# A two-layer graph-attention kernel: the aggregation of five heads as one-pass products of split factors, with the order of work dealt anew

## The chip, the core and the metric

The kernel runs on one core of a Trainium2 chip. The metric is the time of one execution on the device, in microseconds; lower is better. The engines that matter are TensorE (matrix products, with a separate instruction that loads the stationary operand), VectorE, ScalarE, GpSimd, and the DMA queues, of which SP's and GpSimd's are used here.

## The reference

Two layers of graph attention, a residual and a layer norm, over 512 nodes with 768 features. The first layer has eight heads, the second has one.

```python
def gat_layer(x, W, a_s, a_d, b, edge_index, concat):
    n = x.shape[0]
    H, C = a_s.shape
    h = (x @ W).reshape(n, H, C)
    src, dst = (edge_index[0], edge_index[1])
    alpha_s = jnp.einsum('nhc,hc->nh', h, a_s)
    alpha_d = jnp.einsum('nhc,hc->nh', h, a_d)
    e = jax.nn.leaky_relu(alpha_s[src] + alpha_d[dst], NEG_SLOPE)
    m = jax.ops.segment_max(e, dst, num_segments=n)
    e = jnp.exp(e - m[dst])
    denom = jax.ops.segment_sum(e, dst, num_segments=n)
    alpha = e / (denom[dst] + EPS)
    msg = h[src] * alpha[:, :, None]
    out = jax.ops.segment_sum(msg, dst, num_segments=n)
    ...
```

After layer 1 (768 to 8 x 768) comes an ELU, then layer 2 (6144 to 768), then the input is added and every row normalised. The kernel makes a dense 512 x 512 attention matrix out of the edges, so that the sum over messages becomes a matrix product.

## The kernel before

All matrices are 32-bit floats. For each head h there are three families of products on TensorE:

- the projection `M.P*` of the head after the next one (x times that head's part of W1): 15 products instead of 18, by sums and differences of blocks in thirds (`by_thirds`, line 472), four matmuls of 128x128 by 256 columns each;
- the aggregation (`mixed`, line 986): the features `HS[h]` (512 nodes x 768) times the attention matrix, held turned in `PT` (512 x 512). Seven half-size products P1 to P7 are made instead of eight, for three column blocks c, two matmuls each: tokens such as `P50` (product P5, block 0). They need sums of blocks of both factors, made by VectorE: `l0` to `l3` (`left_sums`, into `gS`) and `r0` to `r3` (`right_sums`, into `pS`). The result passes through an ELU into `gT` by ScalarE and VectorE (`fork`, `u`, `w`, `x`, `y`, `n`, `nn`, `N`, `b`, `B`, `f`, `F`);
- the second layer's product `m.P*` (`gT` times that head's part of W2), again 15 products (`second_thirds`, line 552); VectorE adds each to `h2` by `e.P*` (line 560). The sums of `gT` are `g.P*` (`g_thirds`, line 586), some in the spare room of `gS`.

Beside them run, for each next head: logits (`src`, `dst`, VectorE line 422), softmax (`row`, `lift`, `leak`, `rank`, `att`), turning the attention matrix by DMA (`out0` to `out3` are `turn_out`, `in0` to `in3` are `turn_in`), the loads of weights (`d.*` for W1 of the head after next, `t.*` for W2 of the next), the sums of weight blocks (`T.*`, `w.*`, line 200, and additions by GpSimd's DMA queue, line 187), and `back`, which loads sums of x from DRAM into `gT`, since room in the on-chip memory is short.

The order of work is written out by hand. A script is a string of tokens; each token issues its instructions on their engines in the script's order, and each engine works through its own queue in that order. `HEAD[...]` + `SECOND[...]` + `NEXT[...]` make one head; heads 1 to 5 share a script. Buffers come from pools: a tile that is allocated again waits until the last reader of the tile before it in that slot has ended. Products accumulate in PSUM banks that are handed out from a list (`mm`).

The lines of the aggregation's products and of the projection's eviction, which the profile names:

```python
nc.tensor.matmul(st[bank][:, :HN], A_[p][:, k, c * P:(c + 1) * P], B_[p][:, k, :],
                 start=start and k == 0, stop=k == 1, skip_group_check=True)
...
nc.scalar.activation(out(o), ps, AF.Copy, scale=how)
```

Of the kernel before, what the change touches and what calls it, by code (L numbers as in the profile page):

```python
# [8 lines left out]
F32 = mybir.dt.float32  # L9
# [28 lines left out]
def gat_pass(  # L38
# [349 lines left out]
    def left(aT, s):  # L388
# [360 lines left out]
    XA, xsums = left(xT, xS)  # L749
# [161 lines left out]
    parted = {}  # L911

    def turn_out(q, t, rden=None):
        if rden is not None:
            nc.scalar.activation(q, q, AF.Copy, scale=rden)  # L915
        apart = pS[:, t].rearrange("p k n -> p (k n)") if t < 3 else work.tile([P, N], F32, name="nr")
        apart = apart.bitcast(U16)
# [4 lines left out]
    def turn_in(t, copy=nc.scalar.copy):  # L922
        copy(PT.rearrange("p s n -> p (s n)").bitcast(U16).rearrange("p (s n h) -> p s n h", s=NT, h=2)[  # L923
# [25 lines left out]
    def left_sums(h):  # L949
        hs = HS[h]  # L950
        a11, a12, a21, a22 = hs[:, :2, L], hs[:, 2:, L], hs[:, :2, R], hs[:, 2:, R]
        room = xS if h + 1 == H else gS
        s1, s2, s4 = (room.rearrange("p a k n -> p a (k n)")[:, j, :].rearrange("p (k n) -> p k n", k=2)
                      for j in range(3))
# [8 lines left out]
    def right_sums():  # L963
        b11, b12, b21, b22 = PT[:, :2, near], PT[:, :2, far_], PT[:, 2:, near], PT[:, 2:, far_]
        t1, t2, t4 = pS[:, 0], pS[:, 1], pS[:, 2]
# [6 lines left out]
        ]  # L972

    def mixed(h, A_, B_):

        ops = {}
        for c in range(HK):
# [16 lines left out]
            def keep_copy(name, st=st):  # L994
                def f():
                    st[name] = work.tile([P, HN], F32, name=name)
                    nc.scalar.copy(st[name], st["B"][:, :HN])  # L997
                return f
# [11 lines left out]
            def corner(st=st, j=near_j, c=c):  # L1010
                st["nl"] = work.tile([P, HN], F32, name="nl")
                st["zl"] = work.tile([P, HN], F32, name="zl")
# [69 lines left out]

    AA, lsums = left_sums(0)
# [55 lines left out]
    def hold():  # L1139
        forks.extend(mm.tiles.pop() for _ in range(2))  # L1140

    HEAD = ["""d.p12 hold banks P10 fork0 P50 P60 u0 src2 P20 n0 src3 P70 w0 row d.r2 d.r3 d.r1 d.r4 d.r0 d.r5 d.P14 d.p13 d.P13
        d.P12 nn0 d.P1 x0 P11 fork1 P40 b0 P30 y0 f0 P51 dst3 N0 P61 u1 P21 n1 P71 B0 w1 dst2 x1 nn1 N1 P12 fork2 P41 P22 b1
        P31 B1 y1 n2 nn2 P62 F0 u2 N2 w.0 P52 f1 P72 F1 w2 x2 m.P1.0 w.1 P42 lift2 lift0 b2 P32 leak0 m.k0 lift1 m.P1.1 B2 y2
        f2 zero rank0""",
        """P10 P50 w.P10 fork0 src0 P60 u0 P20 src1 n0 row w.P2 P70 w0 x0 nn0 N0 P11 w.P0 fork1 P40 b0 d.r0 d.r1 d.r2 d.r3 d.P1
        d.r4 d.r5 w.P6 d.P14 d.p13 d.P13 d.p12 P30 d.P12 y0 f0 dst0 B0 P51 P61 u1 F0 P21 n1 P71 w1 x1 nn1 dst1 N1 w.P1 P12
        fork2 P41 b1 P31 lift0 y1 f1 leak0 P52 B1 P62 u2 lift1 F1 rank0 P22 n2 P72 g.P9 w2 leak1 g.P12 x2 m.P2 nn2 rank1 N2
# [384 lines left out]
```

## Time and profile before

| | |
|---|---|
| median of 3 runs | 611.2 us (611.05 to 611.65) |
| the profiled execution | 611.07 us, its span 609.3 us |
| TensorE / its weight loads / VectorE / ScalarE / GpSimd busy | 601.4 / 492.8 / 518.1 / 306.2 / 98.9 us |
| TensorE's granted clock | 0.999 |
| bytes moved by DMA | 114.22 MB, mean 187 GB/s |
| one of the heads 1 to 5 | 69.95 to 69.97 us, 324 matmul records |

The span is the time from the first to the last instruction that the profile shows; the rest of the execution's time lies around it. One full-precision matmul of 256 columns stands in the trace as two records. In a grouped row the number after x is the count, then come the busy time in us, the mean of one in ns, and behind the bar the idle time of the engine just before these instructions with what ended it. In a row of the timeline the first number is the start, the second the length in us, and the bracket holds the idle time before.

### The profile page before, as it was taken

To read this page: it belongs to the slowest core of one execution; us is meant where nothing else is said; L and a number is where in the kernel's file an instruction comes from. 1 tells how busy PE (TensorE), PEld (TensorE's weight loads), DVE (VectorE), ACT (ScalarE), POOL (GpSimd) and SP (SyncE) were. 2 spreads that over 40 slices of the span, in tenths; PEclk is the share of its full clock that TensorE was granted. 3 is DMA by queue.
4 is the path that set the end of the run, shared out by engine and by line. 5 is a ranking of instruction groups with operands and counts; after the bars stand their busy time and mean duration, and the time that the engine had idled before them with its cause. 6 is when DMAs were issued, how large, how long until landed. Compare 5 with 4: busy or idle time off the path is not lost.

```text
span 609.3 us, 8356 instructions
## 1 busy us (share of the span) xinstructions
PE 601.4 (99%) x2812; PEld 492.8 (81%) x2812; DVE 518.1 (85%) x1028; ACT 306.2 (50%) x565; POOL 98.9 (16%) x139
## 2 busy tenths in 40 slices
PE   9999999999999999999999999999999999999995
PEld 5665685688888888888888888888888888887863
DVE  7979968779997789868897789977897789989985
ACT  3128776623736166442746056441764247744644
POOL 1210103031300303022300303013110314022000
PEclk9999999999999999999999999999999999999999
DMA  8982898794946949295965959287783949594202
GB/s 293 317 178 78 244 258 221 208 303 76 341 83 219 230 159 265 39 330 99 316 125 153 265 129 305 47 285 156 248 193 79 319 74 287 89 241 71 51 19 107
DMA packets 97342, 114.22 MB, mean 187 GB/s; under 512 B 42966, under 2 KB 78222, under 8 KB 96398
## 3 DMA queue, kind: packets, MB, share of 16 engines
q1 hardware_dynamic: 75230, 89.26, 45.8%
q0 software_dynamic: 21632, 23.79, 24.5%
q10 hardware_dynamic: 432, 0.59, 0.3%
q8 instruction: 23, 0.38, 0.2%
q14 instruction: 25, 0.20, 0.1%
HBM read 99.05 MB, written 2.90 MB: 167 GB/s over the span
## 4 chain that ended last, share of the span: by engine, by line
PE 99%; DVE 0%; ACT 0%; issue 0%; DVEq 0%; ACTq 0%
PE mm L552 22%; PE mm L472 18%; PE mm L986 17%; PE mm L413 12%; PE tr L552 5%; PE bc L986 4%; PE tr L472 4%; PE bc L472 4%; PE tr L986 3%; PE bc L552 3%; PE mm L1348 2%; PE mm L663 1%; PE bc L792 1%; PE tr L1348 1%; PE tr L413 1%; PE bc L271 1%
## 5 line engine op out<-in xcount | busy, mean ns | idle before, releaser
L560 DVE TENSOR_TENSOR h<-h,mm 128x512 f32<-128x512 f32 x74 | 50.4, 681 | 8.9 <-PE mm L552 8.1
L478 ACT ACTIVATE hs<-mm 128x512 f32<-128x512 f32 x26 | 15.5, 597 | 80.5 <-PE mm L472 79.9
L187 POOL DMA_DIRECT2D w2t<-in_L_gnn_W_dram x21 | 28.3, 1664 | 166.1 <-PE mm L472 80.7
L480 DVE TENSOR_TENSOR hs<-hs,mm 128x512 f32<-128x512 f32 x38 | 26.1, 687 | 27.0 <-PE mm L472 19.9
L986 PE MATMUL mm<-PT,hs 128*128 128x256 f32 x192 | 46.6, 380 | 0.0
L552 PE MATMUL mm<-w1r,gT 128*128 128x256 f32 x192 | 44.2, 380 | 0.0
L915 ACT ACTIVATE q<-q,rden 128x512 f32<-128x512 f32 x28 | 20.2, 720 | 42.7 <-DVE rden L899 42.5
L923 ACT COPY PT<-zr 128x1024 uint16<-128x1024 uint16 x35 | 40.4, 1158 | 2.2 <-DMA zr<-pS 1.2
L187 POOL DMA_DIRECT2D w2r<-in_L_gnn_W_dram x14 | 18.3, 1310 | 137.4 <-DVE gT L1038 75.9
L552 PEld LDWEIGHTS mm<-w1r,gT 128*128 128x128 f32 x192 | 36.4, 190 | 5.2 <-DVE gT L589 0.3
L986 PEld LDWEIGHTS mm<-PT,hs 128*128 128x128 f32 x192 | 36.2, 190 | 5.2 <-ACT u L997 0.2
L703 ACT ACTIVATE q<-q,nmax 128x512 f32<-128x512 f32 x36 | 26.0, 723 | 25.9 <-DVE nmax L700 25.9
L472 PE MATMUL mm<-w2r,gT 128*128 128x256 f32 x144 | 33.7, 379 | 0.0
L422 DVE SCALAR_TENSOR_TENSOR scr<-hs,a_s 128x768 bf16<-128x768 f32 x32 | 30.6, 955 | 0.7
L422 DVE SCALAR_TENSOR_TENSOR scr<-hs,a_d 128x768 bf16<-128x768 f32 x32 | 30.5, 952 | 0.3
L472 PEld LDWEIGHTS mm<-w2r,gT 128*128 128x128 f32 x144 | 27.4, 190 | 3.7
L552 PE MATMUL mm<-w1t,gS 128*128 128x256 f32 x128 | 30.2, 379 | 0.0
L472 PE MATMUL mm<-w2r,xT 128*128 128x256 f32 x128 | 29.9, 379 | 0.0
L986 PE MATMUL mm<-pS,gS 128*128 128x256 f32 x120 | 29.3, 379 | 0.0
L918 ACT COPY pS<-q 128x1024 uint16<-128x1024 uint16 x27 | 28.1, 1044 | 0.7
L472 PEld LDWEIGHTS mm<-w2r,xT 128*128 128x128 f32 x128 | 24.3, 190 | 3.3
L552 PEld LDWEIGHTS mm<-w1t,gS 128*128 128x128 f32 x128 | 24.3, 190 | 3.3
(396 smaller groups left out, 1493.9 us busy)
## 6 DMA issues: line engine op xcount, KB each, us to landing
w2r<-in_L_gnn_W_dram SPq DMA_DIRECT2D x48, 384.0 KB
w1r<-in_L_gnn_W_dram SPq DMA_DIRECT2D x43, 384.0 KB
gT<-xd SPq DMA_DIRECT2D x6, 1280.0 KB
w2t<-in_L_gnn_W_dram SPq DMA_DIRECT2D x21, 256.0 KB
w2t<-in_L_gnn_W_dram POOLq DMA_DIRECT2D x21, 256.0 KB, 9.3
w1t<-in_L_gnn_W_dram SPq DMA_DIRECT2D x18, 256.0 KB
w1t<-in_L_gnn_W_dram POOLq DMA_DIRECT2D x18, 256.0 KB, 5.3
w2r<-in_L_gnn_W_dram POOLq DMA_DIRECT2D x14, 256.0 KB, 8.7
```

Of the source, the lines that this page charges most:

```text
L187: return lambda: nc.gpsimd.dma_start(o, part(k, n), accum_op=add)
L413: nc.tensor.matmul(ps[:, :HALF], A_[p][:, k, i * P:(i + 1) * P], B_[p][:, k, :], start=start and k == 0, stop=k == HK - 1, skip_group_chec ...
L422: return [lambda al=al, a=a, sign=sign: nc.vector.scalar_tensor_tensor(scr, HS[h][:, t, :], sign, a, op0=ALU.mult, op1=ALU.mult, accum_out ...
L472: nc.tensor.matmul(bank[chain][:, i * TH:(i + 1) * TH], A_[p][:, k, i * P:(i + 1) * P], B_[p][:, k, :], start=first and i == k == 0, stop= ...
L480: nc.vector.tensor_tensor(out(o), out(o), ps, op=how)
L552: nc.tensor.matmul(bank[chain][:, i * TH:(i + 1) * TH], A_[p][:, k, i * P:(i + 1) * P], B_[p][:, k, :], start=first and i == k == 0, stop= ...
L560: nc.vector.tensor_tensor(out(o), out(o), ps, op=how)
L703: nc.scalar.activation(q, q, AF.Exp, bias=nmax, scale=-1.0, accum_out=dens[t])
L915: nc.scalar.activation(q, q, AF.Copy, scale=rden)
L918: nc.scalar.copy(apart.rearrange("p (h n) -> p h n", h=2), q.bitcast(U16).rearrange("p (n h) -> p h n", h=2))
L923: copy(PT.rearrange("p s n -> p (s n)").bitcast(U16).rearrange("p (s n h) -> p s n h", s=NT, h=2)[:, :, t * P:(t + 1) * P, :], parted.pop( ...
L986: nc.tensor.matmul(st[bank][:, :HN], A_[p][:, k, c * P:(c + 1) * P], B_[p][:, k, :], start=start and k == 0, stop=k == 1, skip_group_check ...
```

## The change

For heads 1 to 5 (`split_heads`) the aggregation is no longer made of seven products. Each factor is split into two parts that the 32-bit one-pass format (float32r) holds exactly: a high part (`aH` for the features, block by block of 128 columns; `bH` for the attention matrix, row block by row block), and what is left (`aL`, `bL`). A third pair (`aD`, `bD`) holds a sum of the two, scaled. For each of the six blocks c, `A{c}` makes eight one-pass matmuls of 128x128 by 512 columns (high x high, rest x rest), `k{c}` scales the bank by 4097 and adds the bias, `D{c}` adds four matmuls of the sums; then `v{c}` (ScalarE, relu and exp) and `G{c}` (VectorE) put the ELU into `gT`. The copies aH, bH are ScalarE's, aL, aD, bL, bD VectorE's.

The parts of a block lie in a room: a tile of 3 x 512 floats from `ring`, which has two. `gS` and `u2` are gone; `g_thirds` takes its spare room from the same ring, allocated by the token `rooms`. `PT`, `pS` and a new `uw` (which also holds the small tiles u, w, nl, zl) become tiles that are allocated anew from head to head; the attention matrix is turned into `raw`, which has uw's slot. `absent` moves into `gT`.

The scripts of heads 0 to 6 are new (`SPLIT_HEAD` for 1 to 4, `LAST_SPLIT_HEAD` for 5, new ones for 0 and 6); head 7 and the second layer (`END`) keep theirs. The diff, cut to what bears on the time:

```diff
-    absent = keep.tile([P, NT, N], BF16, name="absent")
     xS = keep.tile([P, 3, HK, HN], F32, name="xS")
     gT = keep.tile([P, DC, N], F32, name="gT")
+    absent = gT[:, NT:, :].bitcast(BF16).rearrange("p a (b n) -> p (a b) n", n=N)
...
-    def g_thirds():
+    def g_thirds(rooms):

         a = {(i, k): gT[:, k:k + HK + 1:HK, i * TH:(i + 1) * TH] for i in range(2) for k in range(3)}
-        spare = gS.rearrange("p a k n -> p (a k n)")
-        E_ = [square(spare, j) for j in range(4)] + [square(u2.rearrange("p i n -> p (i n)"), 0)]
+        E_ = [square(rooms[j // 3], j % 3) for j in range(4)] + [square(rooms[1][:, D:], 0)]
         G = dict(P2=a[0, 0], P0=a[1, 1], P4=a[1, 2], P9=E_[4], P12=E_[0], P7=E_[1], P1=E_[2], P13=E_[3], P11=a[0, 1],
                  P8=a[1, 0], P10=a[1, 1], P3=a[0, 0], P14=a[0, 2], P5=E_[4], P6=E_[0])
...
-    u2 = late.tile([P, 2, HALF], F32, name="u2")
-    gS = late.tile([P, 3, HK, HN], F32, name="gS")
-    PT = late.tile([P, NT, N], F32, name="PT")
-    pS = late.tile([P, 3, 2, HN], F32, name="pS")
+    ring = ctx.enter_context(tc.tile_pool(name="ring", bufs=2))
     work = ctx.enter_context(tc.tile_pool(name="work", bufs=2))
+    F32R = mybir.dt.float32r
+    split_heads = range(1, 5 + 1)
+
+    def square_tile(name, dtype=F32):
+        return late.tile([P, NT, N], dtype, name=name)
+
+    def pair_of_rooms():
+        return [ring.tile([P, 3 * N], F32, name="room") for _ in range(2)]
+
+    PT, pS, uw, rooms = square_tile("PT"), square_tile("pS"), square_tile("uw"), pair_of_rooms()
+
+    def three_sums(rooms):
+        at = [rooms[0][:, :D], rooms[0][:, D:], rooms[1][:, :D]]
+        return [r.rearrange("p (k n) -> p k n", k=HK) for r in at]
...
-        apart = pS[:, t].rearrange("p k n -> p (k n)") if t < 3 else work.tile([P, N], F32, name="nr")
-        apart = apart.bitcast(U16)
+        apart = pS[:, t].bitcast(U16)
...
-        copy(PT.rearrange("p s n -> p (s n)").bitcast(U16).rearrange("p (s n h) -> p s n h", s=NT, h=2)[
+        to = raw[0] if raw else PT
+        copy(to.rearrange("p s n -> p (s n)").bitcast(U16).rearrange("p (s n h) -> p s n h", s=NT, h=2)[
             :, :, t * P:(t + 1) * P, :], parted.pop(t).rearrange("p (h s d) -> p s d h", h=2, s=NT))
...
+    def uw_part(name, c):
+        return uw[:, ("u", "nl", "zl", "w").index(name), c % 2 * HN:(c % 2 + 1) * HN]
+
+    SPLIT, DOWN = 4096.0, 1.0 - 2.0 ** -13
+
+    def split_left(h):
+
+        parts, ops = {}, {}
+
+        def high(c):
+            def f():
+                parts[c] = ring.tile([P, 3, NT, P], F32R, name="room")
+                nc.scalar.activation(parts[c][:, 0], HS[h][:, :, c * P:(c + 1) * P], AF.Copy, scale=DOWN / SPLIT)
+            return f
+
+        def low(c):
+            return lambda: nc.vector.scalar_tensor_tensor(parts[c][:, 1], parts[c][:, 0].bitcast(F32), SPLIT,
+                                                          HS[h][:, :, c * P:(c + 1) * P], op0=ALU.mult, op1=ALU.subtract)
+
+        def apart(c):
+            return lambda: nc.vector.tensor_tensor(parts[c][:, 2], parts[c][:, 0].bitcast(F32), parts[c][:, 1].bitcast(F32),
+                                                   op=ALU.add)
+        for c in range(DC):
+            ops.update({f"aH{c}": high(c), f"aL{c}": low(c), f"aD{c}": apart(c)})
+        return parts, ops
+
+    def split_right():
+
+        parts, ops = {}, {}
+
+        def of(name, tag):
+            if name not in parts:
+                parts[name] = square_tile(tag, F32R)
+            return parts[name]
+
+        def high(s):
+            return lambda: nc.scalar.activation(of("H", "PT")[:, s], raw[0][:, s], AF.Copy, scale=DOWN)
+
+        def low(s):
+            return lambda: nc.vector.tensor_tensor(of("L", "pS")[:, s], parts["H"][:, s].bitcast(F32), raw[0][:, s],
+                                                   op=ALU.subtract)
+
+        def apart(s):
+            return lambda: nc.vector.scalar_tensor_tensor(of("D", "uw")[:, s], parts["L"][:, s].bitcast(F32), -SPLIT,
+                                                          parts["H"][:, s].bitcast(F32), op0=ALU.mult, op1=ALU.subtract)
+        for s in range(NT):
+            ops.update({f"bH{s}": high(s), f"bL{s}": low(s), f"bD{s}": apart(s)})
+        return parts, ops
+
+    def by_parts(h, A_, B_):
+
+        ops = {}
+
+        def token(c):
+            j, st = h * DC + c, {}
+
+            def first():
+                st["z"] = mm.next()
+                for n, (a, b) in enumerate(((0, "H"), (1, "L"))):
+                    for s in range(NT):
+                        nc.tensor.matmul(st["z"][:, :N], A_[c][:, a, s], B_[b][:, s], start=n == s == 0,
+                                         stop=n == 1 and s == NT - 1, skip_group_check=True)
+
+            def rescale():
+                nc.scalar.activation(st["z"][:, :N], st["z"][:, :N], AF.Identity, bias=b1T[:, j:j + 1], scale=SPLIT + 1.0)
+
+            def last():
+                for s in range(NT):
+                    nc.tensor.matmul(st["z"][:, :N], A_[c][:, 2, s], B_["D"][:, s], start=False, stop=s == NT - 1,
+                                     skip_group_check=True)
+
+            def down():
+                st["n"] = work.tile([P, N], F32, name="nr")
+                nc.scalar.activation(st["n"], st["z"][:, :N], AF.Relu, scale=-1.0)
+                nc.scalar.activation(st["n"], st["n"], AF.Exp, scale=-1.0)
+
+            def up():
+                nc.vector.scalar_tensor_tensor(gT[:, c, :], st["n"], -1.0, st["z"][:, :N], op0=ALU.add, op1=ALU.max)
+                mm.release(st["z"])
+            ops.update({f"A{c}": first, f"k{c}": rescale, f"D{c}": last, f"v{c}": down, f"G{c}": up})
+        for c in range(DC):
+            token(c)
+        return ops

...
+    SPLIT_HEAD = """A0 d.p13 aH3 d.r4 aL3 d.P13 A3 k0 src0 aD3 d.r0 k3 src1 d.r1 w.P2 d.r2 D0 D3 aH1 aL1 aH4 row v0 aL4 aD1 A1 k1
+        dst0 w.P10 A4 D1 aD4 k4 G0 aH2 D4 aH5 w.P6 aL2 aD2 w.P0 d.p12 A2 aL5 v3 v1 G3 aD5 w.P4 k2 v4 w.P1 A5 rooms
+        w.P3 G1 G4 m.P2 w.P7 g.P12 k5 D2 D5 v2 dst1 v5 g.P9 swap e.P2 buffers g.P7 d.r3 d.P12 lift2 lift0 next lift1
+        G2 M.P9 M.P8 m.P9 G5 e.P9 m.P12 g.P13 g.P1 e.P12 M.P13 E.P8 leak0 leak1 g.P11 rank1 m.P0 m.P13 e.P0 d.r5 leak2
+        rank2 out1 g.P10 m.P1 att0 m.P10 e.P13 att2 lift3 T.P2 m.P4 M.P2 E.P9 e.P10 d.P14 out2 g.P8 g.P6 leak3 rank0
+        e.P4 att1 E.P2 d.P1 m.P11 out0 g.P3 t.p13 seed e.P1 rank3 in1 e.P11 d.p11 g.P14 m.P6 e.P6 out3 t.p11 T.P6
+        M.P12 in2 in3 T.P4 m.P3 m.P8 in0 g.P5 T.P7 m.P14 E.P13 T.P10 t.p12 e.P3 T.P0 M.P4 e.P14 m.P5 E.P4 T.P3 bH0 bH1
+        m.P7 E.P12 bL0 T.P1 bH3 aH0 M.P0 bL1 E.P0 M.P6 e.P5 aL0 M.P10 back aD0 bH2 M.P1 bL2 bL3 bD0 bD1 bD3 E.P6 e.P8
+        E.P1 M.P14 M.P5 bD2 t.r5 e.P7 d.P11 E.P14 t.r1 t.r3 E.P10 E.P5 src2 t.P12 M.P11 E.P11 t.r2 M.P7 dst3 M.P3 dst2
+        t.r0 t.r4 t.P13 E.P7 src3 E.P3 t.P14 t.P1 t.P11"""
+    LAST_SPLIT_HEAD = """d.r4 aH3 w.P2 d.p12 A0 aL3 k0 d.r2 d.r1 src0 A3 d.r0 w.P6 D0 d.r3 k3 aD3 D3 src1 aH1 v0 aH4 aL1 aD1 aL4 d.r5
+        G0 A1 A4 v3 aD4 w.P10 k1 D1 w.P0 row k4 G3 aH2 aL2 dst0 D4 v1 aH5 A2 aL5 aD2 A5 w.P1 v4 aD5 k2 G4 G1 k5 rooms
...
+    HEAD = ["""src2 src3 hold P10 banks P12 fork0 P20 row d.r1 n0 P60 d.r5 d.p12 P50 u0 P11 nn0 dst3 fork1 P70 P61 w0 P21 u1
...
+        m.P1.1 lift2 B1 lift1 rank0 d.P14""", *[SPLIT_HEAD] * 4, LAST_SPLIT_HEAD, """w.P10 P10 P12 P11 src0 src1 P51 fork1 P61 fork0 P20 row P60 u1 n0 w.P0 P71 u0 nn0 P70 w0 w1 P50 dst0 w.P6 P40
...
+    REST = ["""F2 buffers leak2 m.P2.0 g.0 g.1 m.k1 lift3 leak1 X.3 X.4 m.P2.1 X.0 X.1 rank1 m.P6.1 g.2 m.P5.1 m.u1 X.5
...
-        ops = mixed(h, AA, BB)
+        ops = by_parts(h, AA, BB) if h in split_heads else mixed(h, AA, BB)
...
-            G, gsums = g_thirds()
-            ops.update(gsums)
+            def rooms_for_g():
+                rooms[:] = pair_of_rooms()
+                G, gsums = g_thirds(rooms)
+                ops.update(gsums)
+                ops.update(second_thirds(h, G, B2))
+            if h in split_heads:
+                ops["rooms"] = rooms_for_g
+            else:
+                G, gsums = g_thirds(rooms)
+                ops.update(gsums)
+                ops.update(second_thirds(h, G, B2))
             ops.update(kept)
-            ops.update(second_thirds(h, G, B2))
-        run(HEAD[0 if h == 0 else 2 if last else 1], ops)
-        if h == 0 and not general:
-            again = nc.values_load(flag[:1, :1], min_val=0, max_val=E)
-        run(SECOND[0 if h == 0 else 2 if last else 1], ops)
-        B2 = B2_next
-        if h == 0:
-            XB = new["X"]
-        if not last:
+
+        def swap():
+            nonlocal PT, pS, uw
+            if h in split_heads:
+                pS = square_tile("pS")
+            if h + 1 in split_heads:
+                raw[:] = [square_tile("uw")]
+            elif h in split_heads:
+                raw.clear()
+                PT, uw = square_tile("PT"), square_tile("uw")
+
+        def following():
+            nonlocal AA, BB, B2, XB
+            B2 = B2_next
+            XB = new.get("X", XB)
+            if last:
+                return
             for n, (m, e) in by_thirds(h + 2, XB, B3).items():
                 ops[f"M.{n}"], ops[f"E.{n}"] = m, e
-            AA, sums3 = left_sums(h + 1)
-            BB, rsums_ = right_sums()
-            ops.update({f"l{j}": f for j, f in enumerate(sums3)})
-            ops.update({f"r{j}": f for j, f in enumerate(rsums_)})
+            if h + 1 in split_heads:
+                AA, left_ops = split_left(h + 1)
+                BB, right_ops = split_right()
+                ops.update(left_ops, **right_ops)
+            else:
+                AA, sums3 = left_sums(h + 1)
+                BB, rsums_ = right_sums()
+                ops.update({f"l{j}": f for j, f in enumerate(sums3)})
+                ops.update({f"r{j}": f for j, f in enumerate(rsums_)})
             ops.update({f"T.{p}": f for p, f in T.items()})
             ops.update(logit_ops(h + 2, (2, 3)))
             ops.update({f"w.{p}": f for p, f in W_.items()})
-            run(NEXT[min(h, 1)], ops)
-            assert all(n.startswith(("w.", "T.q", "in0", "weigh", "part", "turn")) for n in ops), sorted(ops)
-            kept = {n: f for n, f in ops.items() if n.startswith("w.")}
+
+        ops.update(swap=swap, next=following)
+        run(HEAD[h], ops)
+        if h == 0 and not general:
+            again = nc.values_load(flag[:1, :1], min_val=0, max_val=E)
+        run(REST[h], ops)
+        kept = {n: f for n, f in ops.items() if n.startswith(("w.", "aH", "aL", "aD", "src", "dst"))}
```

More of the change, by code (lines that the diff above doesn't have):

```diff
@@ L951, in left_sums @@
         a11, a12, a21, a22 = hs[:, :2, L], hs[:, 2:, L], hs[:, :2, R], hs[:, 2:, R]
-        room = xS if h + 1 == H else gS
-        s1, s2, s4 = (room.rearrange("p a k n -> p a (k n)")[:, j, :].rearrange("p (k n) -> p k n", k=2)
-                      for j in range(3))
+        room = [xS[:, j] for j in range(3)] if h + 1 == H else three_sums(rooms)
+        s1, s2, s4 = (r.rearrange("p k n -> p (k n)").rearrange("p (k n) -> p k n", k=2) for r in room)
         tt = nc.vector.tensor_tensor
@@ L1140, in hold @@
         forks.extend(mm.tiles.pop() for _ in range(2))
[L1142 to L1148, printed above, removed]
-        P42 g.P7 e.P2 b2 m.P9 P32 lift2 w.P4 B2 e.P9 y2 f2 buffers g.P1""",
-        """P10 P50 w.P10 src0 fork0 P60 u0 src1 P20 n0 P70 w0 row loads x0 nn0 w.P6 N0 w.P0 P11 P40 fork1 P30 b0 y0 f0 w.P2 dst0
-        P51 F0 B0 P61 u1 P21 n1 dst1 P71 w1 x1 nn1 w.P1 N1 P12 fork2 w.P4 P41 lift0 b1 P31 y1 f1 leak0 P52 P62 u2 rank0 F1 B1
-        lift1 g.P12 P22 g.P9 P72 leak1 n2 w2 m.P2 x2 nn2 l0 P32 rank1 N2 g.P7 P42 e.P2 y2 m.P9 b2 B2 f2 e.P9 g.P1 out0"""]
```

69 lines of the change are left out of this document (37 added, 32 removed).

## The prediction

> **What bounds the kernel now.** I read the page first (busy shares, granted clock, chain), then what TensorE waited for, then its busy time head by head, then single rows around the aggregation.
>
> ```profile
> span 609.3 us, 8356 instructions
> PE 601.4 (99%) x2812; PEld 492.8 (81%) x2812; DVE 518.1 (85%) x1028; ACT 306.2 (50%) x565; POOL 98.9 (16%) x139
> PEclk9999999999999999999999999999999999999999
> PE 99%; DVE 0%; ACT 0%; issue 0%; DVEq 0%; ACTq 0%
> ```
>
> TensorE is busy for 99% of the span, at the full clock in every slice, and the chain that ended last is TensorE for 99%. The waits of TensorE are one line:
>
> ```profile
> PE bc L271 <- DVE zeros L266: 1.3, 1, 1.3
> ```
>
> It waits once, at the start; after that every product finds its operands. The next view is the busy time of each engine in two heads, 70 us each; the one after it holds only the aggregation's products (line 986) in the second of them.
>
> ```profile
> 212.35:282.32 69.97, 69.97 (x325) 61.31 (x324) 59.45 (x119) 33.87 (x62) 12.16 (x10) 1.00 0.74 194
> 282.32:352.29 69.97, 69.97 (x325) 61.31 (x324) 59.44 (x119) 33.88 (x62) 12.16 (x10) 1.00 0.70 191
> ...
> 282.32:352.29 69.97, 18.62 (x84) 15.87 (x84) 1.00 0.70 191
> ```
>
> After the length the columns are TensorE, its weight loads, VectorE, ScalarE, GpSimd, each with a count, then clock, DMA share, GB/s. A head is 324 matmul records in 69.97 us: 0.216 us for each. The two columns that can grow into a bound are VectorE (59.4 of 70) and the weight loads (61.3 of 70). So the change is worth the TensorE time that it removes, less the waits that it puts between products.
>
> **TensorE's work.** A full-precision product of 128x128 with 256 columns is two records:
>
> ```profile
> 282.32 1.03 PE L986 MATMUL mm<-PT,hs 128*128 128x256 f32 x4
> 283.19 1.03 PE L986 MATMUL mm<-pS,gS 128*128 128x256 f32 x4
> L986 PE MATMUL mm<-PT,hs 128*128 128x256 f32 x192 | 46.6, 380 | 0.0
> L986 PEld LDWEIGHTS mm<-PT,hs 128*128 128x128 f32 x192 | 36.2, 190 | 5.2 <-ACT u L997 0.2
> L271 PE MATMUL bc<-zeros 128*128 128x512 bf16 x7 | 3.2, 630 | 1.3 <-DVE zeros L266 1.3
> ```
>
> Four records start every 0.865 us; one lasts 0.380, so 0.164 of it is the end draining behind the next. A record of 0.216 passes 256 columns twice, which makes 0.216 also the price of 512 columns once, if a one-pass product takes one record. Removed in a split head: 3 column blocks x 7 products x 2 matmuls x 2 records = 84 records. Added: 6 blocks x (8 + 4) matmuls of 512 columns = 72 records. Difference 12 x 0.216 = 2.59 us a head, 12.95 us for five heads. Heads 0, 6 and 7 keep their products.
>
> No row here shows a one-pass 32-bit product. From below I bound it by 0.216 (512 columns at the pace of the rows), from above by two passes, 0.432. The 16-bit products of line 271 also have 512 columns, 0.45 us apart, but they stand at the very start where nothing overlapped. I take 0.216, since all 324 records of a head keep that pace. The Trainium skill, "TensorE: Matmul & The Clock Gate", section "Back-to-back issue gap", gives some 131 ns for 512 columns sustained beside 512/2.4 + 2.5 = 216 ns for an isolated one; the trace stands with the second, and by the first, an estimate, the 72 products would fall from 15.6 to 9.4 us a head.
>
> The weight loads: 72 of 0.190 in place of 84, each still under a record of 0.216. Cover gone, the next product starts about 0.06 later, as after a real wait:
>
> ```profile
> 164.90 0.68 DVE L586 TENSOR_TENSOR gS<-gS,gT 128x512 f32<-128x512 f32 x1
> 165.63 0.51 PEld L552 LDWEIGHTS mm<-w1r,gS 128*128 128x128 f32 x3 [0.17 <-DVE gS L586]
> 165.69 0.63 PE L552 MATMUL mm<-w1r,gS 128*128 128x256 f32 x2
> ```
>
> This row also prices a handover: VectorE ends at 165.58, the load starts 0.05 later, the product another 0.06 later.
>
> **The new waits.** The parts of a factor block c live in a room, and there are two rooms. Block 0 takes one, 3 the other, 1 the first again, and so on: aH1 (ScalarE, the high part) may only write when D0, the last reader of its room, has ended. The order of products is A0 A3 D0 D3 A1 A4 D1 D4 A2 A5 m.P2 D2 D5. The prices:
>
> ```profile
> 282.52 0.60 ACT L478 ACTIVATE hs<-mm 128x512 f32<-128x512 f32 x1 [9.76 <-PE mm L472]
> 290.02 0.63 ACT L1034 ACTIVATE nr<-zr 128x512 f32<-128x512 f32 x1 [0.62 <-DVE zr L1004]
> 288.31 0.69 DVE L200 TENSOR_TENSOR w1r<-w1t,w1r 128x512 f32<-128x512 f32 x1
> 288.91 0.69 DVE L200 TENSOR_TENSOR w1t<-w1r 128x512 f32<-128x512 f32 x1
> 289.51 0.48 DVE L1004 SCALAR_TENSOR_TENSOR zr<-mm,both,u 128x256 f32<-128x256 f32 x1
> 289.90 0.95 DVE L422 SCALAR_TENSOR_TENSOR scr<-hs,a_d 128x768 bf16<-128x768 f32 x1
> 290.78 0.08 DVE L422 DVE_READ_ACCUMULATOR scr<-hs,a_d 128x1 f32 x1
> L915 ACT ACTIVATE q<-q,rden 128x512 f32<-128x512 f32 x28 | 20.2, 720 | 42.7 <-DVE rden L899 42.5
> ```
>
> A 512-column scaled copy on ScalarE is 0.63; on VectorE an operation is 0.69 long, but the next starts after 0.60 (0.39 for 256 columns from PSUM, 0.88 for 768); ScalarE starts 0.04 after TensorE's end, VectorE 0.03 after ScalarE's.
>
> - A1, behind D3. D0 ends 0.16 after D3 starts (the drain). Then 0.04 + aH1 0.63 + 0.03 + aL1 0.69 + 0.05 = 1.60 after D3's start. D3, four records, covers 0.86. Wait 0.74 + 0.06 = 0.80 us. ScalarE and VectorE hold nothing ahead of these two that is still due.
> - A2, behind D4: the same chain from D1. 0.80 us.
> - A3, behind A0. aH3 is queued after E.P3, the eviction of the previous head's last product (the row at 282.52, 0.20 into the head; the next starts 0.50 later). aH3 0.71 to 1.34, aL3 1.38 to 2.06, load 2.11; A0, eight records, ends its issue at 1.73. Wait 0.38 + 0.06 = 0.44 us.
> - A5, behind A2: aL5 stands on VectorE behind aL2, aD2 and w.P0, 0.60 each, and comes 0.15 late: 0.21 us. In head 5 w.P0 stands earlier and this wait is gone.
> - A4: aH4 waits for D3's end, but A1 (1.73) covers the chain. D0 to D5: each rescale k (0.60) and each aD is done while another block's product runs. No wait.
>
> Sum: 0.80 + 0.80 + 0.44 + 0.21 = 2.25 us in heads 1 to 4, 2.05 in head 5, together 11.05 us.
>
> Bounds of this: a guard that holds aH1 only for the readers of the piece it overwrites (A0 reads the high piece, D0 the sum) would leave 1.53 a head, 1.32 in head 5, 7.44 in all; copies at the 0.72 of line 915, whose factor comes from memory, would add 0.09 in each of three waits, 0.27 a head. I take 11.05, the room being allocated as one tile.
>
> **VectorE.** Removed a head, start to start: l0 to l3 4 x 0.87, r0 to r3 4 x 0.60, x and y 6 x 0.40, N and B 6 x 0.33, F 3 x 0.61, together 12.1. Added: six each of aL, aD, G and four each of bL, bD, 26 x 0.60 = 15.6. So 59.4 becomes about 63.0 of a head of 69.6, the lengths summed as the profile sums them.
>
> ```profile
> L957 DVE TENSOR_TENSOR gS<-hs 128x768 f32<-128x768 f32 x7 | 6.7, 950 | 0.0
> L968 DVE TENSOR_TENSOR pS<-PT 128x512 f32<-128x512 f32 x8 | 5.5, 686 | 0.9 <-ACT PT L923 0.8
> L1021 DVE SCALAR_TENSOR_TENSOR gT<-nl,zl 128x256 f32<-128x256 f32 x24 | 10.1, 420 | 1.3 <-ACT nl L1018 1.3
> L1038 DVE SCALAR_TENSOR_TENSOR gT<-nr,zr 128x512 f32<-128x512 f32 x24 | 16.5, 688 | 2.2 <-ACT nr L1035 1.7
> ```
>
> That fits, with 6.6 us to spare, and costs nothing as long as the spare lies where TensorE would otherwise wait. The Trainium skill, "VectorE: DVE Perf Modes", section "The DRAIN you can't avoid", says that the next operation does not start until the pipe is empty, and that one which is not held starts earlier; the row at 288.91 starts 0.09 before its forerunner ended, so the trace shows the second.
>
> **ScalarE, loads, the other moves.** ScalarE gains at most ten copies, six rescales and twelve relu/exp, 20.2 us even at 0.72 each, on 33.9 of 70, before what it loses (forks, u, w, n, nn, b, f): no bound. Bytes of DMA stay the same. On SP's queue d.r4 and d.r0 to d.r2 move ahead of row, the rows that the next head's softmax is made from; lift0 to lift3 read them only behind m.P2, some 18 us into the head, and four loads of 384 KB at the head's mean of 191 GB/s would take 8. On VectorE w.P2 stands ahead of aL1 and reads the sum t.P13, a load and an addition by GpSimd's queue that now go out late in the head before; by the order of the queue I reckon some 9 us from its issue to w.P2, and it lands in 5.3. Cover gone, aL1 and A1 wait as long as it is late. The reload of X parts (back) writes to gT, free after m.P14, and is wanted at M.P1.
>
> ```profile
> GB/s 293 317 178 78 244 258 221 208 303 76 341 83 219 230 159 265 39 330 99 316 125 153 265 129 305 47 285 156 248 193 79 319 74 287 89 241 71 51 19 107
> w2r<-in_L_gnn_W_dram SPq DMA_DIRECT2D x48, 384.0 KB
> gT<-xd SPq DMA_DIRECT2D x6, 1280.0 KB
> w1t<-in_L_gnn_W_dram POOLq DMA_DIRECT2D x18, 256.0 KB, 5.3
> ```
>
> 1280 KB at 191 GB/s (the head's mean) to 341 (the busiest slice) take 3.8 to 6.7 us, and about six products of 1.73, 10.4 us, stand between. Cover gone, its lateness falls on TensorE in full; I take nothing. Heads 0 and 6 are only reordered, without a new wait: zero, with perhaps 0.3 either way.
>
> **Sum.** The profiled execution took 611.07 us for its span of 609.3; 611.07 - 12.95 + 11.05 = 609.2. It lies 0.13 under the median of 611.2, so I forecast the same number for the median.
>
> **Rivals.**
> 1. The waits are smaller (guard by piece, or earlier copies): 611.07 - 12.95 + 7.44 = 605.6. For: the script was dealt with the rooms in view. Against: a room is one tile. With all waits hidden: 598.1.
> 2. Slower by the weight load. If a 512-column one-pass product hides its load less well, each costs a gap. It decides at 1.9 us / 360 products = 5 ns; with the full 0.06 of the row at 165.69 it is 72 x 0.06 x 5 = 21.6, so 630.8. Against: 324 loads a head hide now, with 26 ns to spare each.
> 3. Slower by VectorE: its spare 6.6 us is not where it is needed. Counted without overlap, 0.69 for every 0.60, it comes to some 66.4 plus waits for ScalarE, near 70.2 a head: 612 to 613, and to 615 if a reload is late too. For: the chain aH, aL, aD, G adds eighteen handovers a head.
> 4. The products take two passes, so the change doesn't do what it says: 72 x 0.432 = 31.1 instead of 18.1 a head, +65: 676. Nothing in the trace speaks for or against. The Trainium skill, "FP8 and Floating Point Precision", section "TensorE Precision Notes", has four passes for full 32-bit products and a truncation for the reduced form; the 512 columns per two-pass record agree with the four.
>
> **How the numbers follow.** About 0.2%, 1.2 us, is what can be told from no change: 610.0 and below is faster, above 612.4 slower. Likeliest (chain as reckoned) 0.50, of it 0.36 faster and 0.14 within; smaller waits 0.15, and no waits 0.06, faster; weight load 0.08 and two passes 0.03, slower; VectorE or a late queue 0.18, of it 0.11 slower and 0.07 within. That makes 0.57, 0.21, 0.22. The range 604 to 615 holds the likeliest, the smaller waits and VectorE's case, and leaves out 0.17; the likeliest's own is 607 to 611.
>
> **What would show it.** TensorE's records in a split head fall from 324 to 312, the aggregation's at 0.216 apart. Its waits list A1 and A2 after aL at 0.80 each, A3 at 0.44, A5 at 0.21, VectorE named as releaser. The split heads are 69.6 us from start to start; VectorE's busy column reads about 63. Wrong it is if a record of A lasts another time than 0.38, if gaps stand between the eight products of one A, or if TensorE waits outside of A1, A2, A3 and A5 for more than 1 us a head.

## The result, and the profile after

The changed kernel takes 603.79 us (median of 4 runs, 603.14 to 604.01) beside 611.21 us before (611.05 to 611.65): a ratio of 0.9876, interval 0.9859 to 0.9893. It is 7.4 us faster. The forecast was 609.2, its range 604.0 to 615.0; the sign was right, the size was not, and the median lies just below the range.

From the page of the profiled execution after (604.01 us, span 602.2):

```profile
span 602.2 us, 8248 instructions
PE 594.0 (99%) x2752; PEld 480.5 (80%) x2752; DVE 534.3 (89%) x1043; ACT 323.6 (54%) x555; POOL 99.0 (16%) x139
PEclk9999999999999999999999999999999999999998
PE 99%; DVE 0%; ACT 0%; issue 0%; DVEq 0%; ACTq 0%
```

TensorE is still 99% of the chain that ended last, and no wait of it but the one at the start is listed; its busy time alone fell by 7.4 us, as much as the median. The windows of two split heads, columns as before (length, TensorE, loads, VectorE, ScalarE, GpSimd, clock, DMA share, GB/s):

```profile
210.93:279.43 68.50, 68.50 (x315) 58.78 (x313) 62.81 (x121) 37.54 (x60) 12.92 (x12) 1.00 0.80 199
279.43:347.95 68.52, 68.52 (x314) 58.77 (x313) 62.71 (x121) 37.55 (x60) 11.16 (x11) 1.00 0.80 196
416.45:485.24 68.79, 68.79 (x314) 58.93 (x313) 62.14 (x118) 34.69 (x55) 12.16 (x10) 1.00 0.79 200
485.24:529.27 44.03, 44.03 (x205) 38.73 (x204) 40.30 (x84) 29.63 (x56) 7.29 (x6) 1.00 0.65 147
```

The first two are heads 2 and 3. Each is 1.46 us shorter than the 69.97 before; 2.59 would be the full price of twelve records. VectorE came out at 62.7 to 62.8 (63.0 forecast). The third row is head 5: 68.79, of which 0.19 is only a matter of how the trace places the first one-pass record (below), so 68.6. The fourth is head 6, which is not split; before, the same view gave this:

```profile
492.24:536.70 44.46, 44.46 (x206) 38.43 (x205) 41.10 (x87) 29.81 (x56) 7.29 (x6) 1.00 0.67 153
```

204 records of 0.2159 are 44.04. So head 6 had 0.42 us of gaps before, too short for the list of waits, and its new order has none. Head 0, with the same 0.19 taken into account, is unchanged (71.25 before, 71.28 after). The sum: four heads at 1.46, head 5 at 1.37 and head 6 at 0.43 are 7.6 us. The rest lies before head 0 and behind head 6, in 71.32 and 72.95 us after beside 71.13 and 72.58 before; these parts vary from run to run (below).

Now the products of one split head, head 3 (bc, mm and tr are names of accumulation banks). TensorE and, for the same time, its weight loads (PEld), with the idle time before a load and what ended it:

```profile
279.43 1.27 PE L1044 MATMUL bc<-PT,room 128*128 128x512 f32 x4
280.54 1.08 PE L1044 MATMUL bc<-pS,room 128*128 128x512 f32 x4
281.45 1.07 PE L1044 MATMUL mm<-PT,room 128*128 128x512 f32 x4
282.36 1.07 PE L1044 MATMUL mm<-pS,room 128*128 128x512 f32 x4
283.27 1.07 PE L1052 MATMUL bc<-uw,room 128*128 128x512 f32 x4
284.18 1.20 PE L1052 MATMUL mm<-uw,room 128*128 128x512 f32 x4
285.21 1.10 PE L1044 MATMUL mm<-PT,room 128*128 128x512 f32 x4
286.15 1.08 PE L1044 MATMUL mm<-pS,room 128*128 128x512 f32 x4
...
284.18 0.76 PEld L1052 LDWEIGHTS mm<-uw,room 128*128 128x128 f32 x4 [0.27 <-ACT mm L1048]
285.12 0.76 PEld L1044 LDWEIGHTS mm<-PT,room 128*128 128x128 f32 x4 [0.17 <-ACT room L996]
```

Each row is four products. A0 is the first two rows (its factor rows are PT, the high part, then pS, the rest), A3 the next two, then D0, D3, A1. Two things are to be read here. Four undisturbed products start 0.907 to 0.91 after the four before: 0.227 us each, not 0.216. And A1 starts 1.03 after D3, where the forecast was 0.86 + 0.80. The rows of ScalarE and VectorE for the same stretch say why:

```profile
280.31 0.62 ACT L996 ACTIVATE room<-hs 128x512 fp32r<-128x512 f32 x1
283.47 0.66 ACT L1048 ACTIVATE mm<-mm,b1T 128x512 f32<-128x512 f32 x1 [1.15 <-PE mm L1044]
284.43 0.63 ACT L996 ACTIVATE room<-hs 128x512 fp32r<-128x512 f32 x1 [0.30 <-PE bc L1052]
...
285.10 0.69 DVE L1000 SCALAR_TENSOR_TENSOR room<-room,hs 128x512 fp32r<-128x512 f32 x1 [0.48 <-ACT room L996]
```

The copy aH1 (284.43) does wait for D0 (line 1052), as forecast: the room is guarded as a whole. aL1 on VectorE starts at 285.10, and A1 starts at 285.21, before aL1 ends at 285.79. A1's first four products read only the high part; the rest part is wanted 0.91 later. The wait that is left is another one: D3's first load waits for the rescale k3, which ends at 284.13 (load at 284.18), and D3's second product is 0.11 late (0.336 behind the first, by the record starts).

### The profile page after: what moved, and what is told of

Read it like the earlier page. It is cut to its first block, busy times and chain, and to the rows that moved or that the text cites. A ratio compares the mean times of both kernels' runs of the same rounds, so it can differ in the third digit from the quotient of the medians.

```text
span 602.2 us, 8248 instructions
## 1 busy us (share of the span) xinstructions
PE 594.0 (99%) x2752; PEld 480.5 (80%) x2752; DVE 534.3 (89%) x1043; ACT 323.6 (54%) x555; POOL 99.0 (16%) x139
## 4 chain that ended last, share of the span: by engine, by line
PE 99%; DVE 0%; ACT 0%; issue 0%; DVEq 0%; ACTq 0%
PE mm L553 23%; PE mm L473 18%; PE mm L414 11%; PE mm L1044 7%; PE mm L1080 5%; PE tr L473 5%; PE bc L553 5%; PE mm L1052 4%; PE tr L553 3%; PE bc L473 3%; PE mm L1475 2%; PE bc L1080 2%; PE tr L1080 2%; PE mm L663 1%; PE bc L1044 1%; PE tr L1044 1%
## 5 line engine op out<-in xcount | busy, mean ns | idle before, releaser
L553 PE MATMUL mm<-w1r,gT 128*128 128x256 f32 x176 | 40.4, 379 | 0.0
L928 ACT COPY pS<-q 128x1024 uint16<-128x1024 uint16 x36 | 37.5, 1045 | 0.9
L553 PE MATMUL mm<-w1r,room 128*128 128x256 f32 x160 | 37.5, 379 | 0.0
L553 PEld LDWEIGHTS mm<-w1r,gT 128*128 128x128 f32 x176 | 33.4, 190 | 4.6
L553 PEld LDWEIGHTS mm<-w1r,room 128*128 128x128 f32 x160 | 30.4, 190 | 4.1
L187 POOL DMA_DIRECT2D w1t<-in_L_gnn_W_dram x18 | 23.9, 1479 | 45.9 <-DMA w1t<-in_L_gnn_W_dram 39.4
L934 ACT COPY uw<-zr 128x1024 uint16<-128x1024 uint16 x20 | 22.5, 1156 | 9.8 <-DMA zr<-pS 9.8
L1000 DVE SCALAR_TENSOR_TENSOR room<-room,hs 128x512 fp32r<-128x512 f32 x30 | 20.7, 691 | 7.0 <-ACT room L996 6.8
L695 DVE SCALAR_TENSOR_TENSOR q<-q 128x512 f32<-128x512 f32 x36 | 24.2, 685 | 0.9 <-ACT q L691 0.8
L700 DVE CUSTOM_DVE_ANT_0 q<-q,cnt 128x512 f32<-128x512 f32 x36 | 24.7, 685 | 0.3
```

The costliest lines, as they stand in the source:

```text
L187: return lambda: nc.gpsimd.dma_start(o, part(k, n), accum_op=add)
L553: nc.tensor.matmul(bank[chain][:, i * TH:(i + 1) * TH], A_[p][:, k, i * P:(i + 1) * P], B_[p][:, k, :], start=first and i == k == 0, stop= ...
L700: nc.vector.tensor_tensor_reduce(out=q, in0=q, in1=cnt[:, t, :], scale=1.0, scalar=-NO_EDGE / 2, op0=ALU.add, op1=ALU.min, accum_out=nmax)
L928: nc.scalar.copy(apart.rearrange("p (h n) -> p h n", h=2), q.bitcast(U16).rearrange("p (n h) -> p h n", h=2))
```

## The experiments

Times are medians, beside 610.8 to 611.1 for the kernel before on the same chips. The changed kernel run once more as yardstick:

> The changed kernel once more, as the yardstick for the others of this chip: 603.8 (603.2 to 604.2).

603.36 us (602.51 to 603.84), as expected. The part before head 0, the same in all kernels, took 70.2 to 71.6 us in the profiled executions, so half a microsecond between medians says little; what a split head costs is read from the trace, to some 0.05 us.

**The order of a block's products.**

```diff
-for n, (a, b) in enumerate(((0, "H"), (1, "L"))):
+for n, (a, b) in enumerate(((1, "L"), (0, "H"))):
```

> The eight products of every block A of the split heads in the other order: the four of the rest parts (aL x bL) first, then the four of the high parts (aH x bH). Nothing else changes. Theory 1 (the forecast waits did not come because a block's first four products read only aH, and aL has their 0.91 us to follow): now A1 and A2 wait for aL1 and aL2 as the prediction said. From the changed kernel's rows: aL1 ends 285.79, so A1 could start at 285.90 instead of 285.21 (0.69); aL2 0.62, aL3 0.31, aL5 about 0.1; 1.7 us a head, 8.6 us in all: 612.4 (610.5 to 614), and the five heads are 70.2 from start to start. Rival (the room of two blocks before is not what the copies wait for, or they are early anyway): no change, 603.8.

613.14 us (613.05 to 613.61), slower than before: ratio 1.0036, interval 1.0023 to 1.005. The waits of TensorE in this kernel (total, count, longest), and its head 3:

```profile
PE mm L1044 <- DVE room L1000: 3.6, 8, 0.5
PE tr L1044 <- DVE room L1000: 0.4, 1, 0.4
PE bc L1044 <- DVE room L1000: 0.4, 1, 0.4
...
283.22:353.68 70.46, 69.47 (x315) 58.56 (x313) 62.84 (x121) 37.54 (x60) 11.28 (x11) 1.00 0.77 191
...
288.40 1.18 PE L1052 MATMUL mm<-uw,room 128*128 128x512 f32 x4
290.07 1.20 PE L1044 MATMUL mm<-pS,room 128*128 128x512 f32 x4 [0.49 <-DVE room L1000]
```

Ten waits for aL (line 1000), two in each of the five heads, and a head of 70.46. The same instructions with two groups exchanged cost 9.8 us over the yardstick. The last two rows are D3 and A1: A1 now starts 1.67 after D3, where 0.86 + 0.80 had been forecast and the changed kernel has 1.03. By the record starts, what A1, A2, A3 and A5 lose over 0.227 a product is 0.76, 0.69, 0.37 and 0.08 in this head, beside the 0.80, 0.80, 0.44 and 0.21 of the prediction. So the chain that the prediction reckoned exists, link by link; what it overlooked is that the kernel asks for its last link four products later. That settles this half of the miss.

**What a one-pass product costs.** One kernel with five forms of the four D products, run once (601.96 us, with less work in it than the changed kernel):

```diff
+n, m = {1: (448, P), 2: (N, 64), 4: (384, P), 5: (256, P)}.get(h, (N, P))
+wt, mv = A_[c][:, 2, s, :m], B_["D"][:, s, :n]
+if h == 3:
+    wt, mv = (t_.bitcast(BF16).rearrange("p (n two) -> p n two", two=2)[:, :, 1] for t_ in (wt, mv))
```

> Measures what sets the 0.227 us from one one-pass product to the next; the four D products of each block take another form in each head, so the output differs in heads 1, 2, 4 and 5 by what they leave out and in head 3 by the shorter format. Head 1: 448 of 512 moving columns; head 2: 64 of 128 stationary columns; head 3: the same tiles read as 16-bit; head 4: 384 moving columns; head 5: 256. A products stay as control at 0.227. Theory column (each 32-bit column read costs 0.443 ns): 448 gives 0.198, 384 0.170 or the weight load's 0.19, head 2 0.227, head 3 0.227 or 0.216. Theory fixed (0.213 for 512 columns and 13 ns an instruction): 448 gives 0.200, head 2 0.227. Theory load (the load of 0.188 and a handover of 0.039 set the pace): 448, 384 and 256 all stay at 0.227, head 2 falls to 0.216, and head 3 with a shorter load falls too.

Rows of the timeline with four D products each, and what follows them; then the weight loads grouped by form (count, busy, mean ns):

```profile
160.12 0.97 PE L1056 MATMUL tr<-uw,room 128*128 128x448 f32 x4
160.92 1.02 PE L473 MATMUL mm<-w2r,xT 128*128 128x256 f32 x4
...
364.86 0.86 PE L1056 MATMUL mm<-uw,room 128*128 128x384 f32 x4
365.56 1.46 PE L473 MATMUL tr<-w2r,xT 128*128 128x256 f32 x6
...
214.63 1.09 PE L1056 MATMUL mm<-uw,room 128*64 128x512 f32 x4
215.56 1.12 PE L1056 MATMUL tr<-uw,room 128*64 128x512 f32 x4
...
L1056 PEld LDWEIGHTS mm<-uw,room 128*128 128x128 f32 x48 | 7.9, 188 | 2.6 <-ACT mm L1048 2.0
L1056 PEld LDWEIGHTS mm<-uw,room 128*64 128x64 f32 x20 | 2.6, 134 | 1.8 <-ACT mm L1048 0.3
L1056 PEld LDWEIGHTS <-room 128*128 128x128 bf16 x24 | 2.2, 97 | 3.0 <-issue 0.3 <-DVE w1t L200 0.3
```

448 columns: the four starts from 160.12 to 160.92 are 0.202 apart before rounding. 384 columns: 0.70 / 4 = 0.175. With 256, single starts mostly stand 0.119 apart (0.113 behind a longer product). What streaming alone takes is read from full-precision records, taken as two passes over their columns: with 512 columns their starts are 0.4293 apart (in the run below), with 256 columns 0.2159; the 256 columns more, twice, are 512 in 0.2134, and 2.5 ns of a record are left over. That is 0.187, 0.160 and 0.107 for the 448, 384 and 256 columns here, and the products take 12 to 16 ns more each time. Theory fixed holds. Theory load falls: 64 stationary columns load in 0.134 instead of 0.188, 16-bit ones in 0.097, and the first keep 0.23, the second 0.225. Theory column falls with the 384 columns (0.170 by it) and the 256 (0.113); the 448 lie too near to both theories to tell.

The second kernel on this question alternates A0 and A3 product by product in heads 1 to 4, and makes D in head 2 of full-precision products:

```diff
+work_ = [(c, st["z"])] if not (h < 5 and c == 3) else [(0, held.pop()), (3, st["z"])]
 ...
+if h == 2:
+    wt, mv = wt.bitcast(F32), mv.bitcast(F32)
```

> Two questions on the 13 ns that a one-pass product costs over its 512 columns. In heads 1 to 4 the products of A0 and A3 alternate, so that two products that follow one another go to different banks; in head 2 the D products are full-precision ones with the same 512 columns, which adds 24 x (2 x 0.43 - 0.23) = 15 us there. Theory accumulation (a product waits for the one before on the same bank): the 16 alternating products come at 0.216, the others stay at 0.227. Theory fixed (it belongs to the one-pass product): they stay at 0.227, and the full-precision records of head 2 come at 2 x 213.3 + 2.6 = 0.429 each.

Rows of alternating products, then of head 2's D products:

```profile
300.85 0.39 PE L1049 MATMUL bc<-pS,room 128*128 128x512 f32 x1
301.07 0.39 PE L1049 MATMUL mm<-pS,room 128*128 128x512 f32 x1
301.30 0.39 PE L1049 MATMUL bc<-pS,room 128*128 128x512 f32 x1
...
220.22 1.45 PE L1060 MATMUL mm<-uw,room 128*128 128x512 f32 x3
221.51 2.74 PE L1060 MATMUL tr<-uw,room 128*128 128x512 f32 x6
```

Products that go to two banks in turn (bc, mm, bc) still come 0.227 apart: theory accumulation falls. The full-precision records with the same tiles and 512 columns come 1.29 / 3 = 0.43 apart, two passes and 2.5 ns. So some 13 ns belong to a one-pass product, whatever its columns, its load and its bank; what in the chip takes them stays open. Every one of these products has a new stationary operand; none that keeps it was run, so a fixed price of the change is not excluded. The whole run, a single one, was 626.5 us, 23 above the yardstick: 24 x (0.86 - 0.23) = 15 from head 2's passes, and 2 a head in heads 1 to 4, where the alternating products wait for aH3 and the rescale.

**The gaps that are left.** The rescale of blocks 3 and 4 on 128 columns:

```diff
+n = P if c in (3, 4) else N
-nc.scalar.activation(st["z"][:, :N], st["z"][:, :N], AF.Identity, ...
+nc.scalar.activation(st["z"][:, :n], st["z"][:, :n], AF.Identity, ...
```

> The rescale of blocks 3 and 4 (k3, k4) works on 128 columns instead of 512, so three quarters of these two blocks are left unscaled. Theory 1 (the two gaps of 0.11 us left in a head, at D3 and D4, are the wait for k3 and k4, which end 0.05 before the late weight load): both gaps go, 2 x 0.11 x 5 = 1.1 us: 602.7 (602.3 to 603.1). Rival (the gap is that of a change of bank or tile): no change, 603.8, and the pitch of 0.336 stays at the second product of D3 and D4.

603.06 us (602.86 to 603.38), as if the theory held; the trace says otherwise. Heads 1 to 4 take 68.41 to 68.50, in the mean 0.05 less than 68.51, and not 0.22:

```profile
283.60 1.07 PE L1053 MATMUL mm<-uw,room 128*128 128x512 f32 x4
284.54 1.19 PE L1044 MATMUL mm<-PT,room 128*128 128x512 f32 x4
...
283.86 0.63 ACT L996 ACTIVATE room<-hs 128x512 fp32r<-128x512 f32 x1 [0.62 <-PE bc L1053]
```

The gap has left D3 (1.07 for its four, 1.20 above) and stands in A1 (1.19), which now waits for aH1: 283.86 + 0.63 = 284.49, load and product at 284.54. Two chains of 0.9 us stand one behind the other. The copies alone in two pieces:

```diff
+for s in ((slice(0, 2), slice(2, NT)) if c in (1, 2) else (slice(0, NT),)):
+    nc.scalar.activation(parts[c][:, 0, s], HS[h][:, s, c * P:(c + 1) * P], AF.Copy, scale=DOWN / SPLIT)
```

> Only the copies aH1 and aH2 are made in two pieces, so that the first two products of A1 and A2 need half the copy. Theory balance (two chains of 0.9 us follow one another: D3 and D4 wait 0.11 us for the rescale, and this wait just covers aH1 and aH2): nothing, 603.4 (603.0 to 603.8), the gaps at D3 and D4 stay. Rival (A1 and A2 are late by the copy alone): 602.5.

603.42 us (602.38 to 603.79), heads 1 to 4 at 68.48 to 68.54: nothing, as theory balance has it. Both together:

> The copies aH1 and aH2 in two pieces and the rescale of blocks 3 and 4 on 128 of 512 columns (three quarters of them stay unscaled). Theory balance: with both chains short no gap is left, a split head falls from 68.5 to 68.2 (312 records: 240 of 0.216 and 72 of 0.227), 1.1 to 1.5 us in five heads: 602.1 (601.7 to 602.5). Rival (something else is next, as aL1 on VectorE): gaps stay, 603 or more.

603.13 us (602.60 to 603.29), heads 1 to 4 at 68.32 to 68.42: 0.14 a head, not 0.3. A third chain comes next, aL1 behind aH1, and the second half of A1 waits for it:

```profile
285.60 1.15 PE L1045 MATMUL mm<-pS,room 128*128 128x512 f32 x4
...
285.55 0.76 PEld L1045 LDWEIGHTS mm<-pS,room 128*128 128x128 f32 x4 [0.21 <-DVE room L1001]
...
284.80 0.69 DVE L1001 SCALAR_TENSOR_TENSOR room<-room,hs 128x512 fp32r<-128x512 f32 x1 [0.57 <-ACT room L997]
```

aL1 ends at 285.49; the load that needs it comes at 285.55, held up by line 1001, and its four products spread over 1.15 instead of 1.07. Rescale, high part and rest part each take what one group of four products covers, and to shorten one hands the gap to the next.

**Two versions meant to be faster.** The rescale of blocks 3 and 4 half on ScalarE and half on VectorE, with the copies in pieces:

```diff
+n = HN if c in (3, 4) else N
+nc.scalar.activation(st["z"][:, :n], st["z"][:, :n], AF.Identity, bias=b1T[:, j:j + 1], scale=SPLIT + 1.0)
+if n < N:
+    nc.vector.tensor_scalar(st["z"][:, n:N], st["z"][:, n:N], SPLIT + 1.0, b1T[:, j:j + 1], op0=ALU.mult, op1=ALU.add)
 ...
```

> Two waits shortened together, nothing left out. The rescale of blocks 3 and 4 is dealt to two engines (ScalarE 256 columns, VectorE 256; two sums of weight blocks on VectorE's queue move behind it), and the copies aH1 and aH2 are made in two pieces, so that a block's first products start after half the copy. Theory 1 (in the changed kernel D3 and D4 wait 0.11 us for the rescale, and where that is taken away A1 and A2 wait as long for aH1 and aH2, since both chains are 0.9 us): with both shortened the gaps go, 2 x 0.11 x 5 = 1.1 us less: 602.7 (602.3 to 603.1), a split head 68.3. Rival (a gap of that size comes back wherever the chain is longest next, aL1 and aL2 behind VectorE's longer queue): 603.8 or more, and the trace shows the gap at the second half of A1 or A2.

607.93 us (607.50 to 608.26), 4.6 us slower than the yardstick:

```profile
285.25 0.45 ACT L1050 ACTIVATE mm<-mm,b1T 128x256 f32<-128x256 f32 x1 [1.15 <-PE mm L1045]
285.73 0.49 DVE L1052 TENSOR_SCALAR mm<-mm,b1T 128x256 f32<-128x256 f32 x1 [0.81 <-ACT mm L1050]
```

The halves did not run side by side: VectorE starts its half 0.03 after ScalarE ended, and the row names ScalarE's instruction, on the same bank, as what it waited for. Whether the shared bank is the reason was not tested. The rescale ends at 286.22, 0.97 after its start, in place of 0.66. By the record starts of head 3, D3 and D4 are now late by 0.43 each in place of 0.11, and the second half of A1, which needs aL1 from VectorE, by 0.24: 0.9 us a head, the 4.6 in five heads. Head 6 split as well:

```diff
-split_heads = range(1, 5 + 1)
+split_heads = range(1, 6 + 1)
-*[SPLIT_HEAD] * 4, LAST_SPLIT_HEAD, """w.P10 P10 P12 P11 ...
+*[SPLIT_HEAD] * 5, """aH3 w.P2 A0 aL3 k0 src0 A3 w.P6 D0 aD3 k3 D3 ...
 ...
```

> Head 6 is split as well (head 5 takes the order of heads 1 to 4, head 6 that of the last split head without the projection). Theory 1 (the gain of a split head is 12 records of 0.216 less 72 times 13 ns less 0.2 of waits, wherever the head stands): head 6 falls from 44.03 to 42.6 us, head 5 from 68.8 to 68.5: 603.8 - 1.7 = 602.1 (601.6 to 602.7). Rival (head 6 has no projection beside it, so the softmax of head 7 or VectorE comes late, and head 7 waits): 604 or more, with waits of TensorE in the first products of head 7.

611.90 us (611.28 to 612.68): the rival. Head 6 lasts 50.42:

```profile
484.47:534.89 50.42, 43.72 (x194) 35.72 (x192) 44.54 (x86) 30.42 (x49) 8.96 (x8) 0.99 0.65 142
PE mm L1080 <- ACT PT L934: 4.7, 1, 4.7
```

VectorE has 44.5 us of work there, more than TensorE's 42.6 would be; the softmax of head 7 falls behind and its first product waits 4.7 us for the turned attention matrix. Head 6 is 6.2 us longer than in the changed kernel (0.19 of the 50.42 is again the placing of its first record), and what follows it takes 75.7 us in place of 72.4 to 73.0. Head 6 has no projection, so VectorE has 40.3 of 44.0 before the split adds anything. Both versions together:

> The two changes before together: head 6 split, the rescale dealt to two engines and the two copies in pieces in all split heads. If both act and do not meet: 603.8 - 1.1 - 1.7 = 601.0 (600.4 to 602.0). If the gaps only move, 602.1.

617.71 us (616.57 to 618.26), some 14.4 above the yardstick, where the two losses of 4.6 and 8.5 make 13.1: they add up, and a little more. None of these beats the changed kernel.

**One head alone.**

```diff
-split_heads = range(1, 5 + 1)
+split_heads = range(1, 1 + 1)
-*[SPLIT_HEAD] * 4, LAST_SPLIT_HEAD,
+LAST_SPLIT_HEAD, *[OLD_HEAD] * 4,
 ...
```

> One part of the change alone: only head 1 is split (with the order that the change gives to head 5); heads 2 to 5 keep the seven products and the order of before; heads 0 and 6 have the new orders. Theory 1 (the gain is that of each split head, 69.97 - 68.50 = 1.47 us, and the new orders of heads 0 and 6 give nothing): 611.2 - 1.5 = 609.7 (609.3 to 610.1). Rival (the new orders of heads 0 and 6 carry part of it): 608 or less.

608.87 us (608.35 to 609.29), 2.2 us below the kernel before, where 1.5 was expected: below the range that the theory gave, and not as low as the rival's. The trace accounts for 1.6: head 1 is 68.98 - 0.19 = 68.79 (1.18 less), heads 2 to 5 are back at 69.97, and head 6 has the 44.03 of its new order (0.43 less). The other 0.6 fits the part before head 0 (70.16, 71.13 in the profile of before), which varies from run to run. The gain belongs to the split head, and 0.4 of it to head 6's order.

## Why the prediction missed, point by point

**TensorE's records: right in number.** 240 + 72 records stand in a head, as reckoned.

**The price of a one-pass product: mis-sized.** 0.216 was taken from the two-pass records, on the ground that all 324 keep that pace; those bear 2.5 ns each over their columns, the one-pass product 13. Undisturbed ones come at 0.227, the 72 of a head at 0.229 in the mean without the two gaps of 0.11: 72 x 0.0134 = 0.96 us a head, 4.8 in all, lost from the 12.95. No row of the kernel before shows a one-pass product in a warm stream. The nearest, line 271, was read wrong: its seven products start 0.427 apart (0.45 is their busy time through seven) and last 0.63, so they do overlap. The products of line 300 start 0.213 apart right behind them and 0.109 later in the same run, so that stretch ran at half the later pace, and the row read so gives 0.213 for 512 columns, without the 13 ns. Rival 2 had set the limit at 5 ns a product; 13 is beyond it, though not by the weight load that it named. The Trainium skill, "TensorE: Matmul & The Clock Gate", section "Back-to-back issue gap", by which 512 columns would come each 131 ns when sustained, is contradicted once more: 72 in a head, none below 0.22; its isolated 216 is nearer.

**The new waits: wrong.** 2.25 us a head were forecast at A1, A2, A3 and A5; none of the four came. The step that failed is "D0 ends ... + aH1 0.63 + 0.03 + aL1 0.69": aL was put ahead of the block's first product, though the code hands the high parts to the first four. With the four products' 0.91 as cover for aL, only aH has to be there at the block's start: A1's load comes at 284.43 + 0.63 + 0.05 = 285.11 and D3's issue ends at 285.21, so the two are in balance, and A3 has time to spare (aH3 ends at 280.93, A3 starts at 281.45). "D0 to D5: ... No wait" was wrong the other way: from A3's last issue to D3's load it is 0.16 of drain, 0.04, the rescale's 0.66 (not 0.60) and 0.05, which is all of D0's 0.91, and k3 and k4 (in head 5 k5 too) cost 0.11 each.

**The two errors have opposite signs.** Waits 11.05 forecast, about 1.2 measured (two of 0.11 in four heads, three in head 5): 9.8 too much. Products: 4.8 too little. Heads 0 and 6: 0.4 not foreseen. 609.2 - 9.8 + 4.8 - 0.4 = 603.8, the measured median; that it agrees to the tenth is luck, since the parts outside these heads vary by more. The right sign was luck as well: with the waits as forecast, the true price of the product would have made it 609.2 + 4.8 = 614.0, slower than before. The rival "all waits hidden", given 598.1 and 0.06, had the waits nearly right and would have missed by the price of the product.

**Right:** the whole room as guard (line 996 waits for line 1052), VectorE's 63, ScalarE and the loads as no bound. "Its spare 6.6 us is not where it is needed" did not come in heads 1 to 5; it did in a split head 6. (The 66.4 of that rival does not follow from its rows: 0.09 more for each of the 26 added operations makes 65.3.)

## What to carry to other kernels

Before a chain of copies is charged to a group of products, look at which product of the group reads its last link: here the order of two loops was worth 9.8 us. A price taken from another form of the same instruction needs its own bounds; 13 ns on each of 360 products took more than a third of the gain. When several chains are equally long, shortening one moves the gap to the next, and the median alone may look as if it had helped.

## What was not expected of the hardware

A one-pass product costs 12 to 16 ns beyond its columns (0.119, 0.175, 0.202, 0.227 for 256, 384, 448 and 512 columns), 16-bit ones of 512 columns 0.225, a full-precision record 2.5 ns (0.43 for two passes of 512). The first one-pass record behind a full-precision one is placed 0.03 after it and the next 0.42 later; the two together, 0.445, are an ordinary pair, so the gap is none. Behind a gap of 0.11, and at the start of a split head, the next products come unevenly, at 0.224 to 0.239 (0.232 in the mean of the thirteen behind D3's gap in head 3), before they settle at 0.227; why stays open.
